# Sharing one sum of products between neighbouring pixels, in one batch of four, in a stack of location-dependent convolutions

## The chip, the cores and the metric

The kernel runs on one core of one Trainium2 chip. The metric is the time of one execution on the device in microseconds (us). A comparison counts from about 0.2% upwards.

## What is computed

Four layers work on an input of 4 batches, 32 x 32 pixels and 16 channels. Each layer normalises its input (a group norm over pairs of channels) and adds its result to it. The first three layers have this form, and nearly all of the work is in their `second` term: for each of the 1024 output pixels (i, j) there is a 3 x 3 convolution of its own, `K`, which runs over the whole image of every batch.

```
first = jnp.einsum('ijpq,bpqc->bijc', M2, inputs)
K = jnp.transpose(G, (2, 3, 4, 0, 1, 5)).reshape(kh, kw, c, h * w * f)
shifted = lax.conv_general_dilated(inputs, K, window_strides=(1, 1), padding='SAME', ...)
shifted = shifted.reshape(b, h, w, h, w, f)
diff = jax.nn.relu(inputs[:, :, :, None, None, :] - shifted)
second = jnp.einsum('ijpq,bpqijc->bijc', W2, diff)
return first - L * second
```

The fourth layer is a long filter that the kernel applies as products with a Toeplitz matrix.

## The kernel before, in words

A **block** is 8 output pixels with 16 channels each, so 128 columns of weights. A layer has 128 blocks. A **pass** is one block with one batch, and its result is a PSUM tile `pt` of 128 x 1024 values, two banks of 512. There are 3 x 128 x 4 = 1536 passes. Since relu(x - s) is -min(s - x, 0), the identity is taken off the middle tap of the weights (L495, on GpSimd), and one VectorE instruction per pass (L591, `scalar_tensor_tensor`) takes the minimum with 0, multiplies by `Wp` and adds up along the row into `acc`.

TensorE makes a pass out of six matmuls (L583). The upper and lower 64 rows of the array each work on one half of the 1024 positions, beside each other. Each half has 64 rows of input: four taps of 16 channels (weights `ga`), four more taps (`gb`), both in plain fp32 over 512 columns, and the ninth tap (`gn`) in fp32r over 480 columns. In the ninth, weights and image are each split into a high and a low piece, and the four products of pieces fill the 64 rows. In the records, one fp32 matmul shows as two weight loads and two matmuls, one fp32r matmul as one of each; so a pass has 10 records of each kind (`ga` 4, `gb` 4, `gn` 2).

PSUM is a ring of four such `pt` tiles[...]. The blocks of a layer are taken in groups of 8 (`GC`), in this order: the first 8 blocks for batches 0 and 1, the same for batches 2 and 3, then the blocks between, each for all four batches, and the last 8 again by pairs of batches. So the image of one pair of batches can be made while the other pair is worked on.

Beside that, short pieces of other work are written as generators, and `step()` advances each of them by one piece after each pass: the norm and the image of the next layer (`make_image`, `store_image`, `load_image`), which write the normalised image to DRAM and read it back shifted by the taps, on the queues of SP, ACT and POOL in turn (32 transfers for a pair of batches); the `first` term (L437); the filter of layer 4. The weights are fetched per 8 blocks by three transfers on SP's queue (L480), the middle tap is changed by GpSimd (L495), and the ninth tap is split by ScalarE (L499) and VectorE (L503). `Wp` comes by SP's queue (L522), 1 MB for two blocks, into a ring of six tiles.

Layer 0 starts from an array `raw` that the host has laid out by taps, so that its images are only loaded and normalised in place (`load_first`, `first_images`). Layer 4's Toeplitz tiles are loaded during layer 3 into `TB` = 5 tiles and some more, all but one of them.

Of the kernel before, what the change touches and what calls it, by code (L numbers as in the profile page):

```python
# [7 lines left out]
F32 = mybir.dt.float32  # L30
# [7 lines left out]
P = 128  # L38
B, C, S = 4, 16, 32
NBLK = 128  # L40
TAPS = [0, 1, 3, 4, 8, 5, 6, 7, 2], [0, 1, 3, 4, 2, 5, 6, 7, 8]
ROW = 2 * 4 * 34
RUN = ROW - 2
NINE = 2 * 4 * 32
GC = 8
# [7 lines left out]
TB = 5  # L53
# [3 lines left out]
def conv_stack_kernel(ctx, tc, x, raw, M, W, first_w, G, h0, coef, cst, dft, idp, idq, out):  # L57
# [8 lines left out]
    gp = ctx.enter_context(tc.tile_pool(name="gp", bufs=2))  # L66
    gs = ctx.enter_context(tc.tile_pool(name="gs", bufs=2))
# [12 lines left out]
    cs = const.tile([P, P + C + 2], F32, name="cs")  # L80
    nc.sync.dma_start(out=cs, in_=cst)
    nc.scalar.dma_start(out=xs, in_=x)
    avg, mid = cs[:, :P], cs[:, P : P + C]
    avg_r = const.tile([P, P], F32R, name="avg_r")
    is_lo, sign = cs[:, P + C : P + C + 1], cs[:, P + C + 1 :]

    ys, ye, img = [], [], []  # L90
    for a in range(2):
        ys.append(const.tile([P, ROW + 2 * NINE], F32, name=f"y{a}"))
        ye.append(const.tile([P, ROW + 2 * NINE], F32, name=f"e{a}"))
        img.append(dram.tile([10, C, ROW + 2 * NINE], F32, name=f"img{a}"))
# [6 lines left out]
    half_blks = NBLK // 2  # L101

# [73 lines left out]
    def image_tiles(a):  # L176


        ims[a] = [
            imp.tile([P, *shape], d, tag=f"im{a}{k}", name=f"im{a}{k}")  # L180
            for k, (d, shape) in enumerate(
                ((F32, (4, 2, 4, 34)), (F32, (4, 2, 4, 34)), (F32R, (2, 4, 4, S)))
            )
        ]

    def load_first(a, which, b=slice(0, 2)):

        if a not in ims:
            image_tiles(a)
            nine[a] = st.tile([P, 2, 4, 4, S], F32, name=f"nine{a}")  # L190
        src = raw[:, a, 4 * ROW * which :][:, : 4 * (NINE if which == 2 else ROW)]
        if which == 2:
            nc.sync.dma_start(
                out=nine[a][:, b].rearrange("p b l cc x -> p (b l cc x)"),
                in_=src[:, b.start * 2 * NINE : b.stop * 2 * NINE],
            )
            return
        to = ims[a][which]
        nc.sync.dma_start(
            out=to[:, :, b].rearrange("p l b cc x -> p l (b cc x)"),  # L200
            in_=src.rearrange("p (l b n) -> p l b n", l=4, b=2)[:, :, b].rearrange(
                "p l b n -> p l (b n)"
            ),
        )

    def first_images():


        of = lambda t, b: t[:, :, b % 2].rearrange("p l cc x -> p l (cc x)")
        rlo = st.tile([P, B], F32, name="rlo")  # L210

        def center(b):
            v = of(ims[b // 2][1], b)
            nc.scalar.activation(v, v, AF.Identity, bias=neg[:, b : b + 1])

        def scale(b):
            v = of(ims[b // 2][1], b)
            nc.scalar.activation(v, v, AF.Copy, scale=rstd[:, b : b + 1])

        def clear(which, a, b=slice(0, 2)):  # L220

            top, bottom = (0, 0, slice(0, S)), (3, 3, slice(0, S))
            t = ims[a][which].bitcast(F32)
            if which == 2:
                t = t.rearrange("p b l cc x -> p l b cc x")
            left, right = ((slice(0, 4), slice(0, 4), slice(x, x + 1)) for x in (0, S - 1))
            parts = {
                0: [(g, g + 16, left) for g in range(0, P, 32)] + [(0, 32, top)],
                1: [(g, g + 32, right) for g in (0, 64)]
                + [(g + 32, g + 48, left) for g in (0, 64)]  # L230
                + [(96, P, bottom)],
                2: [(0, P, right)],
            }[which]
            for lo, hi, (l, cc, x) in parts:
                nc.gpsimd.memset(t[lo:hi, l, b, cc, x], 0.0)  # L235

        def first_tap(b, which=0):
            v = of(ims[b // 2][which], b)
            nc.vector.tensor_scalar(v, v, neg[:, b : b + 1], rstd[:, b : b + 1], ALU.add, ALU.mult)  # L239

        def last_tap(b):

            v, v8 = (
                t[:, b % 2].rearrange("p l cc x -> p (l cc x)") for t in (nine[b // 2], ims[b // 2][2])
            )
            m = neg[:, b : b + 1]
            nc.vector.tensor_scalar(v8, v, m, rstd[:, b : b + 1], ALU.add, ALU.mult)
            yield
            nc.vector.tensor_scalar(v, v, m, rlo[:, b : b + 1], ALU.add, ALU.mult)
            yield  # L250
            nc.vector.scalar_tensor_tensor(v8, v8.bitcast(F32), sign, v, ALU.mult, ALU.add)
            clear(2, b // 2, slice(b % 2, b % 2 + 1))
# [14 lines left out]
        first, second = prepare_g(0, 0, halves[0], nc.vector), prepare_g(0, 0, halves[1])  # L267
        tables = [coefs[:, at : at + 2 * P].rearrange("p (r n) -> p r n", r=2) for at in soon_at]
        def dft(ch, ri):
            coefficient_dft(dfts[ch], ab, tables[ch], ri)  # L270
# [4 lines left out]

# [3 lines left out]
        norm = group_norm(xs, as_it_is, group_sums)  # L279
        next(norm)  # L280
        next(first)
        next(first)
# [3 lines left out]
        next(first)  # L286
# [7 lines left out]
        at = [slice(b % 2, b % 2 + 1) for b in range(B)]  # L294
# [4 lines left out]
        center(0)  # L299
        scale(0)  # L300
        for ch in range(1, SOON):
            result(ch)
        first_tap(0)
        clear(0, 0, at[0])
        clear(1, 0, at[0])
        nc.vector.tensor_scalar(rlo, rstd, is_lo, None, ALU.mult)
        list(first)
        list(last_tap(0))
        for which in range(2):
            first_tap(1, which)  # L310
            clear(which, 0, at[1])
        list(last_tap(1))
        next(second)

        def rest():

            yield
            yield
            list(second)
            yield  # L320
            center(2)
            center(3)
            clear(1, 1)
            yield
            for _ in range(3):
                yield
            for b in (2, 3):
                scale(b)
                first_tap(b)
                clear(0, 1, at[b])  # L330
                yield
                yield from last_tap(b)
                yield
            for a in range(2):
                normalise(a, xs[:, 2 * a : 2 * a + 2], *(t[:, 2 * a : 2 * a + 2] for t in (neg, rstd)))
                yield

            nc.vector.tensor_copy(avg_r, avg)

        todo.append(rest())  # L340

    def normalise(a, xt, neg, rstd):
        yc[a] = work.tile([P, 2, NBLK], F32, tag=f"yc{a}", name=f"yc{a}")
        for b in range(2):
            at = slice(b, b + 1)
# [67 lines left out]
    def first_term(layer, xt):  # L413

        ft = work.tile([P, 2, 8, S], F32, tag="ft", name="ft")
        with tc.tile_pool(name="mp", bufs=4) as mp:
# [15 lines left out]
            for _ in range(GC - 4):  # L432
                yield
# [699 lines left out]
```

## Time and profile before

| | us |
|---|---|
| median of 3 runs (3060.91 to 3060.95) | 3060.93 |
| the profiled execution, its own time | 3061.04 |
| its span, first to last instruction | 3059.2 |
| TensorE busy by the records | 3049.9 |
| VectorE busy | 2066.2 |
| GpSimd busy | 245.9 |
| ScalarE busy | 74.8 |

The page gives the busy time of each engine, the span in 40 slices, the DMA queues, the chain of work that ended last, the costliest groups (line, engine, operation, tiles, shapes, count, busy time, mean of one in ns, idle time before it and its releaser), and the DMA issues. The ends of matmuls are modelled, so their start times are to be trusted and their durations are not. A timeline merges neighbouring records of one kind into a row: start, time from the start of the first to the end of the last, and how many.

### The profile page before, as it was taken

How to read it: one execution, taken by the hardware profiler on the slowest of the kernel's cores; microseconds unless marked ns; L12 is line 12 of the kernel's file. 1: busy time of each engine (PE TensorE's matmuls, PEld its weight loads, DVE VectorE, ACT ScalarE, POOL GpSimd, SP SyncE). 2: the span in 40 equal slices, each digit the busy share in tenths (PEclk: the TensorE clock that was granted, in tenths of full speed). 3: DMA queues.
4: the chain of work that ended last, by engine and by line, in shares of the span. 5: the costliest groups of instructions: out<-in, count | busy, mean ns of one | idle time of the engine just before them, and what ended most of it. 6: DMA issues, size and time to landing. Idle time of an engine off the chain costs nothing.

```text
span 3059.2 us, 39208 instructions
## 1 busy us (share of the span) xinstructions
PE 3049.9 (100%) x16268; PEld 2080.0 (68%) x16268; DVE 2066.2 (68%) x3358; ACT 74.8 (2%) x97; POOL 245.9 (8%) x288
## 2 busy tenths in 40 slices
PE   9999999999999999999999999999999999999999
PEld 5656556788766885678876555588567887655554
DVE  7667766666667776666666666777666766666664
ACT  1000000000000000000000000000000000000000
POOL 1022320000000201000000000020100000000000
PEclk9999999999999999999999999999999999999999
DMA  7353443333432745333433343274544444445422
GB/s 236 101 148 90 111 116 94 90 90 97 104 90 62 159 131 131 90 90 97 103 90 90 97 104 90 62 156 131 143 101 99 102 115 107 97 96 119 99 41 43
DMA packets 72218, 322.20 MB, mean 105 GB/s; under 512 B 10920, under 2 KB 21160, under 8 KB 46696
## 3 DMA queue, kind: packets, MB, share of 16 engines
q1 hardware_dynamic: 60464, 302.09, 39.5%
q10 hardware_dynamic: 7112, 9.93, 1.8%
q0 software_dynamic: 4464, 7.68, 1.2%
q8 instruction: 127, 2.08, 0.3%
q14 instruction: 51, 0.42, 0.1%
HBM read 313.46 MB, written 6.20 MB: 104 GB/s over the span
## 4 chain that ended last, share of the span: by engine, by line
PE 99%; DVE 0%; DMA 0%; issue 0%; ACT 0%; POOL 0%; ACTq 0%; DVEq 0%
PE pt L583 97%; PE pt L863 1%; PE pt L437 1%; DMA g<-in_G_dram 0%; DVE junk L591 0%; PE pt L690 0%; PE pt L731 0%; PE pt L617 0%; POOL im L235 0%; DVE im L239 0%; DVE gn L503 0%; ACT gn L499 0%; DVE st L142 0%; ACT L781 0%; DVE x L606 0%
## 5 line engine op out<-in xcount | busy, mean ns | idle before, releaser
L591 DVE SCALAR_TENSOR_TENSOR junk<-pt,w 128x1024 f32<-128x1024 f32 x1536 | 1880.9, 1225 | 945.6 <-PE pt L583 923.8
L583 PE MATMUL pt<-im,ga 64*128 64x512 f32 x6144 | 1941.8, 588 | 0.1
L583 PE MATMUL pt<-im,gb 64*128 64x512 f32 x6144 | 1940.7, 588 | 0.0
L583 PE MATMUL pt<-im,gn 64*128 64x480 f32 x3072 | 1574.2, 778 | 0.0
L583 PEld LDWEIGHTS pt<-im,gb 64*128 64x128 f32 x6144 | 916.6, 186 | 418.0 <-issue 294.3
L583 PEld LDWEIGHTS pt<-im,ga 64*128 64x128 f32 x6144 | 919.6, 185 | 174.4 <-issue 68.8
L583 PEld LDWEIGHTS pt<-im,gn 64*128 64x128 f32 x3072 | 509.2, 186 | 334.9 <-issue 270.0
L495 POOL TENSOR_TENSOR ga<-ga,cs 128x1024 f32<-128x1024 f32 (+1 forms) x48 | 112.6, 2346 | 1990.3 <-DMA ga<-in_G_dram 1990.1
L591 DVE DVE_READ_ACCUMULATOR junk<-pt,w 128x1 f32 x1536 | 127.3, 83 | 0.0
L503 DVE TENSOR_TENSOR gn<-g,gn 32x1024 fp32r<-32x1024 f32 (+2 forms) x98 | 117.7, 1201 | 2.8 <-ACT gn L499 0.6
L499 ACT CAST gn<-g 128x1024 fp32r<-128x1024 f32 (+2 forms) x49 | 50.4, 1028 | 2225.5 <-PE pt L583 2120.0
L452 POOL DMA_DIRECT2D fd<-ft x48 | 25.3, 534 | 314.8 <-ACT ft L444 302.4
L863 PE MATMUL pt<-t,y 128*32 128x512 f32 (+3 forms) x352 | 23.9, 432 | 0.0
L405 POOL DMA_DIRECT2D im<-img x44 | 22.3, 513 | 17.2 <-DMA img<-y 9.8
L746 POOL COPY hs<-v 32x512 f32<-32x512 f32 x16 | 17.1, 1071 | 46.4 <-ACT v L740 45.8
L863 PEld LDWEIGHTS pt<-t,y 128*32 128x32 f32 x352 | 10.9, 110 | 12.8 <-issue 10.9
L987 DVE TENSOR_TENSOR xo<-xo,both 128x512 f32<-128x512 f32 x2 | 1.4, 692 | 23.7 <-DMA both<-sd 23.7
L661 POOL TENSOR_TENSOR H<-H,d 128x256 f32<-128x256 f32 x8 | 6.8, 849 | 91.1 <-DVE d L666 90.8
L863 PE MATMUL pt<-t,yp 128*32 128x512 f32 (+3 forms) x192 | 13.6, 434 | 0.0
L378 POOL COPY e<-y 32x204 f32<-32x204 f32 (+1 forms) x8 | 3.6, 481 | 117.4 <-ACT y L375 117.4
L863 PEld LDWEIGHTS pt<-t,yp 128*32 128x32 f32 x192 | 6.1, 110 | 7.4 <-issue 6.2
L437 PE MATMUL pt<-mt,yt 128*64 128x512 f32 x48 | 11.0, 598 | 0.0
(107 smaller groups left out, 197.9 us busy)
## 6 DMA issues: line engine op xcount, KB each, us to landing
w<-in_W_dram SPq DMA_DIRECT2D x188, 1024.0 KB, 7.2
g<-in_G_dram SPq DMA_DIRECT2D x47, 512.0 KB, 7.8
ga<-in_G_dram SPq DMA_DIRECT2D x47, 512.0 KB, 3.6
gb<-in_G_dram SPq DMA_DIRECT2D x47, 512.0 KB, 6.4
mt<-in_M_dram SPq DMA_DIRECT2D x12, 512.0 KB, 8.3
w<-in_M_dram SPq DMA_DIRECT2D x12, 512.0 KB, 3.7
t<-hd ACTq DMA_DIRECT2D x28, 160.0 KB, 7.0
t<-hd SPq DMA_DIRECT2D x28, 160.0 KB, 8.1
```

Source lines behind the costliest of these rows:

```text
L378: nc.gpsimd.tensor_copy(e[96:, :, 1:, :], v[96:, :, :3, :])
L405: (nc.sync, nc.scalar, nc.gpsimd)[n % 3].dma_start(out=out, in_=src.rearrange("l c x -> c l x"))
L437: nc.tensor.matmul(pf[64 * h : 64 * h + 64], lhsT=yt[:, k].rearrange("k b c -> k (b c)"), rhs=mt[:, bass.ts(h, 512)], start=(k == 0), stop ...
L452: nc.gpsimd.dma_start(out=fv[h, cc, b], in_=ft[at : at + C, cc])
L495: engine.tensor_tensor(gv, gv, mid.unsqueeze(1).to_broadcast([P, gv.shape[1], C]), ALU.subtract)
L499: nc.scalar.copy(gn, g9)
L503: nc.vector.tensor_tensor(lo, g9[r : r + 32], lo.bitcast(F32), ALU.subtract)
L583: nc.tensor.matmul(pt[:, half, px], lhsT=w[rows, blk % GC, :], rhs=rhs, start=n == 0, stop=n == 2,)
L591: nc.vector.scalar_tensor_tensor(junk, pt.rearrange("p h m -> p (h m)"), 0.0, wt, ALU.min, ALU.mult, accum_out=acc[b // 2][:, b % 2, blk : ...
L661: mul = lambda o, u, w: nc.gpsimd.tensor_tensor(o, u, w, ALU.mult)
L746: nc.gpsimd.tensor_copy(hs[quarter[u], :, bass.ts(c, 8)], v[quarter[c], bass.ts(u, 8)].rearrange("q p m -> q m p"),)
L863: nc.tensor.matmul(rows.rearrange("n (j r) -> n j r", j=C)[:, :, 8 * cc :], lhsT=y(cc).rearrange("p q b -> p (q b)"), rhs=ts[k][q][:, :, : ...
```

## The change

Pixels are taken in pairs of neighbours along a row. Call the left one's inputs x0, x1, x2 and the right one's x1, x2, x3, and a row of taps g0, g1, g2. With S = g0 + g1 + g2, the left sum is S·x1 + g0·(x0 - x1) + g2·(x2 - x1), and the right sum, over x1, x2, x3, is S·x1 + g1·(x2 - x1) + g2·(x3 - x1). So one product S·x1 per row of taps serves both pixels, and each has two products of its own.

- Batches 0 to 2 keep six matmuls per pass (`direct`), with other taps in the fours and with even and odd pixels apart.
- Batch 3 uses `shared`: six fp32r matmuls of 256 columns for the three S·x1, into a PSUM tile `both`; ScalarE copies `both` to SBUF (`sb`); then for even and for odd pixels six matmuls of 256 columns each into `pt`: two of four taps in fp32, four of one tap in fp32r. VectorE adds `sb` to `pt` in place, and the instruction with the minimum follows as before. A shared pass takes two tiles of the PSUM ring.
- The weights come per 4 blocks (`GC` = 4) in `prepare_g`: GpSimd changes the middle tap and makes S, ScalarE and GpSimd split S and the third tap into pieces, GpSimd's queue writes the pieces to DRAM by eight transfers, and SP's queue reads them back into six tiles by nine; the six tiles are double buffered. A list of pairs of passes (`units`, `first_need`, `last_use`) says when each begins.
- `raw` is gone: layer 0 makes its images as the other layers do, through DRAM. An image of batches 0 and 1 takes 36 transfers, one of batches 2 and 3 takes 76. `make_image` is spread over more steps.
- `TB` is 3; three Toeplitz tiles are loaded inside the last stage.

The core of the diff:

```diff
-TAPS = [0, 1, 3, 4, 8, 5, 6, 7, 2], [0, 1, 3, 4, 2, 5, 6, 7, 8]
-ROW = 2 * 4 * 34
-RUN = ROW - 2
-NINE = 2 * 4 * 32
-GC = 8
+SHARED = (False, False, False, True)
+FOURS = [[0, 3, 6, 5], [1, 4, 7, 8]], [[0, 3, 6, 5], [1, 4, 7, 2]]
+PX = 4 * S
+JOB = 8
+GC = 4
...
+    gs = ctx.enter_context(tc.tile_pool(name="gs", bufs=3))
+    gn = ctx.enter_context(tc.tile_pool(name="gn", bufs=2))
+    ge = ctx.enter_context(tc.tile_pool(name="ge", bufs=1))
...
+    units = []
+    for layer in range(3):
+        ends = range(JOB), range(NBLK - JOB, NBLK)
+        units += [(layer, blk, a) for a in range(2) for blk in ends[0]]
+        units += [(layer, blk, a) for blk in range(JOB, NBLK - JOB) for a in range(2)]
+        units += [(layer, blk, a) for a in range(2) for blk in ends[1]]
+    last_use = {}
+    for n, (layer, blk, _) in enumerate(units):
+        last_use[(layer * NBLK + blk) // GC] = n
...
+    def image_tiles(layer, b):
+        tile = lambda name, d, *shape: imp.tile([P, *shape], d, tag=f"{name}{b}", name=f"{name}{b}")
+        if SHARED[b]:
+            ims[layer, b] = [
+                tile("f", F32, 4, 2, 64),
+                tile("n", F32R, 4, 2, 64),
+                *(tile(name, F32R, 4, 64) for name in ("m", "v", "s0", "s1", "s2")),
+            ]
+        else:
+            ims[layer, b] = [tile("f", F32, 4, 2, PX), tile("n", F32R, 4, PX)]
...
+                v = yp[a][:, b].rearrange("p cc (m k) -> p cc m k", k=2)
+                here, after, m = v[:, :, :16, 1], v[:, :, 1:, 1], v[:, :, :, 0]
+                row = ys[:, b, : 9 * 64].rearrange("p (k cc m) -> p k cc m", k=9, m=16)
+                nc.gpsimd.tensor_tensor(row[:, 1], m[:, :, 1:], here, ALU.subtract)
+                nc.gpsimd.tensor_tensor(row[:, 2], after, here, ALU.subtract)
+                nc.gpsimd.tensor_tensor(row[:, 0], m[:, :, :16], here, ALU.subtract)
+                whole = ys[:, b, 64:192]
+                hi, lo = ys[:, b, 192:384], ys[:, b, 384:576]
+                yield
+                nc.scalar.copy(hi[:, 128:].rearrange("p (cc m) -> p cc m", m=16).bitcast(F32R), here)
+                yield
+                nc.scalar.copy(hi[:, :128].bitcast(F32R), whole)
+                nc.gpsimd.tensor_tensor(
+                    row[:, 8], here, hi[:, 128:].rearrange("p (cc m) -> p cc m", m=16), ALU.subtract
+                )
+                yield
+                nc.gpsimd.tensor_tensor(lo[:, :128], whole, hi[:, :128], ALU.subtract)
+                edges.append((b, row))
...
+    def prepare_g(q, wait=3):
+        layer, ch = divmod(q, NBLK // GC)
+        raw = ge.tile([96, 3, 2 * P], F32, tag="raw", name="raw")
+        nc.sync.dma_start(out=raw.rearrange("r k n -> r (k n)"), in_=E[layer][ch])
+        f = gs.tile([P, 2, GC * P], F32, tag="f", name="f")
+        nc.sync.dma_start(out=f.rearrange("r k n -> r (k n)"), in_=F[layer][ch])
+        yield
+        for _ in range(wait):
+            yield
+        fv = f[:, 1].rearrange("r (n f) -> r n f", f=C)
+        rv = raw[:, 1].rearrange("r (n f) -> r n f", f=C)
+        for v, m in ((rv, mid_e), (fv, mid)):
+            nc.gpsimd.tensor_tensor(
+                v, v, m.unsqueeze(1).to_broadcast([v.shape[0], v.shape[1], C]), ALU.subtract
+            )
+        for k in (1, 2):
+            nc.gpsimd.tensor_tensor(raw[:, 0], raw[:, 0], raw[:, k], ALU.add)
+        for _ in range(wait):
+            yield
+        both = raw[:, 0::2]
+        hi, lo = (ge.tile([96, 2, 2 * P], F32R, tag=tag, name=tag) for tag in ("hi", "lo"))
+        nc.scalar.copy(hi, both)
+        yield
+        nc.gpsimd.tensor_tensor(lo, both, hi.bitcast(F32), ALU.subtract)
+        to = gd[q % 3]
+        for k, t in enumerate((hi, lo)):
+            for u in range(2):
+                for slot in range(2):
+                    nc.gpsimd.dma_start(
+                        out=to[slot, :, k, :, bass.ts(u, 2 * P)],
+                        in_=t[48 * u : 48 * u + 48, slot].bitcast(F32),
+                    )
+        yield
+        while q > 1 and now["unit"] <= last_use[q - 2]:
+            yield
+        tiles = [gn.tile([P, GC * P], F32R, tag=f"g{n}", name=f"g{n}") for n in range(6)]
+        gt[q] = f, *tiles
+        for n, (slot, *dys) in enumerate(((1, 0, 2), (1, 2, 0), (1, 1), (0, 0), (0, 1), (0, 2))):
+            for half, dy in enumerate(dys):
+                rows = slice(64 * half, 64 * half + 64) if len(dys) > 1 else slice(0, P)
+                src = to[slot, dy].rearrange("k c n -> (k c) n")
+                nc.sync.dma_start(
+                    out=tiles[n][rows].bitcast(F32),
+                    in_=src.unsqueeze(0).to_broadcast([4 // len(dys), 32, GC * P]),
+                )
...
+    def shared(layer, blk, b):
+        f, n, m, v, *ws = gt[(layer * NBLK + blk) // GC]
+        at = bass.ts(blk % GC, P)
+        fi, ni, mi, vi, *sums = ims[layer, b]
+        both = pair_psum()[:, :, :256]
+        for dy, (w, t) in enumerate(zip(ws, sums)):
+            for half in range(2):
+                rows = slice(64 * half, 64 * half + 64)
+                nc.tensor.matmul(
+                    both[:, half],
+                    lhsT=w[rows, at],
+                    rhs=t[rows].rearrange("p l m -> p (l m)"),
+                    start=dy == 0,
+                    stop=dy == 2,
+                )
+        sb = small.tile([P, 2, 256], F32, tag="both_sb", name="both_sb")
+        nc.scalar.copy(sb, both)
+        pt = pair_psum()
+        taps = ((f[:, 0], fi[:, :, 0]), (n, ni[:, :, 0]), (m, mi)), ((f[:, 1], fi[:, :, 1]), (n, ni[:, :, 1]), (v, vi))
+        for k in range(2):
+            for j, (w, t) in enumerate(taps[k]):
+                for half in range(2):
+                    rows = slice(64 * half, 64 * half + 64)
+                    nc.tensor.matmul(
+                        pt[:, half].rearrange("p (r k m) -> p k r m", k=2, m=16)[:, k],
+                        lhsT=w[rows, at],
+                        rhs=t[rows],
+                        start=k == j == 0,
+                        stop=k == 1 and j == 2,
+                    )
+        v = pt.rearrange("p h (r k m) -> p (h r) k m", k=2, m=16)
+        nc.vector.tensor_tensor(
+            v,
+            v,
+            sb.rearrange("p h (r m) -> p (h r) m", m=16).unsqueeze(2).to_broadcast([P, 32, 2, 16]),
+            ALU.add,
+        )
+        return pt
+    def run_unit(n, acc):
+        layer, blk, a = units[n]
+        now["unit"] = n
+        for b in (2 * a, 2 * a + 1):
+            pt = (shared if SHARED[b] else direct)(layer, blk, b)
+            junk = junkp.tile([P, S * S], F32, tag="junk", name="junk")
+            nc.vector.scalar_tensor_tensor(
+                junk,
+                pt.rearrange("p h m -> p (h m)"),
+                0.0,
+                wts[64 * layer + blk // 2][:, blk % 2, :],
+                ALU.min,
+                ALU.mult,
+                accum_out=acc[a][:, b % 2, blk : blk + 1],
+            )
+            step()
...
+    first_need = {}
+    for q in range(2, 3 * NBLK // GC):
+        first_need.setdefault(last_use[q - 3] + 1 if q > 2 else 0, []).append(q)
...
-        w = np.asarray(inputs[f"L{i}_conv_Wp"]).reshape(4, 8, S, 4, 8, S)
-        w = w.transpose(0, 2, 1, 4, 3, 5).reshape(64, 2, 8, S * S).transpose(0, 2, 1, 3)
+        w = np.asarray(inputs[f"L{i}_conv_Wp"]).reshape(4, 8, S, 4, 8, S // 2, 2)
+        w = w.transpose(0, 2, 1, 4, 3, 6, 5).reshape(64, 2, 8, S * S).transpose(0, 2, 1, 3)
...
+        g = g.transpose(0, 2, 3, 4, 1, 5).reshape(NBLK // GC, GC, 9, C, P)
+        fours = [[g[:, :, taps].transpose(0, 2, 3, 1, 4) for taps in half] for half in FOURS]
+        fours = np.stack([np.stack(half, 3) for half in fours], 1)
+        arrays[f"F{i}"] = fours.reshape(NBLK // GC, P, 2 * GC * P)
+        e = g.reshape(NBLK // GC, 2, GC // 2, 3, 3, C, P).transpose(0, 1, 3, 5, 4, 2, 6)
+        arrays[f"E{i}"] = e.reshape(NBLK // GC, 96, 3 * GC // 2 * P)
...
-    held, last = (1, 0, 7, 6, 5, 4, 3), 2
-    after = (3, 7, 6, 5, 4)
+    held, last = (1, 7, 6, 0, 5), 2
+    after = (7, 6, 5, 4, 3)
...
-        if n == 2:
-            list(load_toeplitz(last, toeplitz_tile(last, tp)))
+        if n in (2, 4, 5):
+            k = {2: 4, 4: 3, 5: last}[n]
+            list(load_toeplitz(k, toeplitz_tile(k, tp)))
```

## Prediction

> **What bounds the kernel now.** I read the page's busy times first, then the chain of work that ended last, then the groups.
>
> ```profile
> PE 3049.9 (100%) x16268; PEld 2080.0 (68%) x16268; DVE 2066.2 (68%) x3358; ACT 74.8 (2%) x97; POOL 245.9 (8%) x288
> ...
> PE 99%; DVE 0%; DMA 0%; issue 0%; ACT 0%; POOL 0%; ACTq 0%; DVEq 0%
> ...
> L591 DVE SCALAR_TENSOR_TENSOR junk<-pt,w 128x1024 f32<-128x1024 f32 x1536 | 1880.9, 1225 | 945.6 <-PE pt L583 923.8
> L583 PE MATMUL pt<-im,ga 64*128 64x512 f32 x6144 | 1941.8, 588 | 0.1
> L583 PE MATMUL pt<-im,gn 64*128 64x480 f32 x3072 | 1574.2, 778 | 0.0
> L583 PEld LDWEIGHTS pt<-im,gn 64*128 64x128 f32 x3072 | 509.2, 186 | 334.9 <-issue 270.0
> L503 DVE TENSOR_TENSOR gn<-g,gn 32x1024 fp32r<-32x1024 f32 (+2 forms) x98 | 117.7, 1201 | 2.8 <-ACT gn L499 0.6
> L495 POOL TENSOR_TENSOR ga<-ga,cs 128x1024 f32<-128x1024 f32 (+1 forms) x48 | 112.6, 2346 | 1990.3 <-DMA ga<-in_G_dram 1990.1
> ```
>
> The chain is TensorE from end to end, and the conv matmuls never wait (idle 0.1 us over 6144). VectorE waits 924 us for them. So TensorE's time per pass decides. Matmul ends are modelled, so I take starts. In the timeline of TensorE and of its weight loads, a usual pass:
>
> ```profile
> 15.26 1.02 PE L583 MATMUL pt<-im,ga 64*128 64x512 f32 x4
> 16.12 1.02 PE L583 MATMUL pt<-im,gb 64*128 64x512 f32 x4
> 16.58 0.78 PE L583 MATMUL pt<-im,gn 64*128 64x480 f32 x2
> 17.20 0.59 PE L583 MATMUL pt<-im,ga 64*128 64x512 f32 x2
> ```
> ```profile
> 16.55 0.19 PEld L583 LDWEIGHTS pt<-im,gn 64*128 64x128 f32 x2 [0.24 <-issue]
> 16.98 0.41 PEld L583 LDWEIGHTS pt<-im,ga 64*128 64x128 f32 x4 [0.24 <-issue]
> ```
>
> A pass takes 17.20 - 15.26 = 1.94 us (1536 of them: 2980 us, the chain's 97%). `ga` to `gb` is 0.86: two records per half, 0.43 each, both halves beside each other. `gb` to the next `ga` is 1.08, so the ninth tap has 1.08 - 0.86 = 0.22. An fp32 record sends its 512 columns twice (0.43 / 1024 = 0.42 ns a column); at that rate 480 columns are 0.20. The slot is longer than its columns. The next weights' load starts with the ninth's matmul (16.12 + 0.86 = 16.98), and their matmul comes 0.22 later. Now two other places: fp32 matmuls of 256 columns (their loads), and a tiny fp32r matmul (8 columns) with `ga` behind it.
>
> ```profile
> 320.14 0.94 PEld L617 LDWEIGHTS pt<-coefs,table 64*128 64x128 f32 x8
> ```
> ```profile
> 1021.67 0.16 PE L122 MATMUL pt<-pieces,avg_r 64*128 64x8 f32 x1
> 1021.70 0.67 PE L583 MATMUL pt<-im,ga 64*128 64x512 f32 x1
> ```
> ```profile
> 1021.68 0.51 PEld L583 LDWEIGHTS pt<-im,ga 64*128 64x128 f32 x4
> ```
>
> L617's eight loads are (0.94 - 0.19) / 7 = 0.107 apart, the halves in turn: 0.215 per half, as long as 2 x 256 columns. After L122, `ga` really begins at 1021.70 + 0.67 - 0.59 = 1021.78, only 0.10 after its load. So a load costs 0.10 when its half of the array stands empty, and nothing I find is shorter than 0.215 when a matmul is running in it.
>
> **What the Trainium skill says.** "TensorE: Matmul & The Clock Gate", section "LDWEIGHTS (loading the stationary operand)", prices a load by its columns at 1.2 GHz: 107 ns for 128. The 0.10 above agrees. Its section "Back-to-back issue gap" says that load and matmul together set the spacing, and gives some 81 ns for 128 columns where the matmul alone would be 56; the trace has no such stream, but the 0.22 for 480 columns points the same way. "TensorEngine Tiling (Array Packing)", "Key Properties": tiles load and multiply in parallel. The trace agrees: the halves' loads show as one row of 0.19 for two.
>
> **The change, part by part** (against the profiled 3061.04 us, of which 3059.2 span; the median, 3060.93, is the same).
>
> *Passes of batches 0 to 2* keep two fp32 matmuls and one fp32r of 480 columns per half: 1.94, no change.
>
> *Passes of batch 3*, 384 of them. Per half: three fp32r matmuls of 256 columns, then twice one fp32 matmul (two records) and two fp32r. That is 4 fp32 records at L617's 0.215 = 0.86, and 7 fp32r slots. No row shows an fp32r matmul of 256 columns in a stream. From below it is its columns, 256 x 0.42 = 0.107; from above the load's 0.216 (the ninth tap's slot, which is longer than its columns). I take 0.216: in the ninth tap the load, not the columns, seems to end the slot, and here every load begins under a matmul. 7 x 0.216 + 0.86 = 2.37, so 2.37 - 1.94 = +0.43 x 384 = **+167 us**. At 0.107 it would be 1.61: -0.33 x 384 = -127. In columns alone the change saves a sixth of a pass; it has 22 loads per pass where there were 10.
>
> *VectorE*: +384 additions of 128 x 1024 out of PSUM, nearest row L591, 1.23 each: +472; L503's 118 go to GpSimd. 2066 + 472 - 118 = 2420 us. Per block 4 x 1.33 + 1.23 = 6.6 beside TensorE's 3 x 1.94 + 2.37 = 8.2: hidden. Where only batches 2 and 3 run (16 blocks a layer), 3.9 beside 4.3: hidden still. With a short shared pass (1.61) TensorE needs 3.55 there: 48 blocks x 0.35 = 17 us lost.
>
> *ScalarE*: +384 copies of 128 x 512, some 0.58 by the row of L632: hidden by the second part of the pass (1.7). *PSUM*: a shared pass takes two of four tiles; the copy frees the first, and the next use of it is two direct passes later.
>
> *Weights*, per 4 blocks (33 us): GpSimd 3 additions of 256 and two of 512 per row, by L495's 2.3 ns an element 4 us, and eight DMA issues at 0.53 (as L452), 4 us: 8 of 33. SP gets 11 issues of some 0.35. Bytes per block grow from 0.72 to about 1.2 MB, in packets of 1 to 4 KB; the DMA share goes from some 0.4 to 0.6. `Wp` is asked for 8 blocks ahead. ScalarE's split waits for GpSimd, which waits for the fours, which wait for TensorE's end with the tile three groups back; behind it on ScalarE stand the copies for VectorE. It comes 8 passes (16 us) after the issue, against 8 for landing (`g` 7.8) and 4 for GpSimd: covered by 4 us. Uncovered, it would cost what it is late, once per 4 blocks. Cost taken: nothing.
>
> *Start*. Conv matmuls begin at 10.66 now. Then: norm ready at 9.2, image to its store 3.7 (between the same steps at 992.7 and 996.35 now), store 2.6, 18 transfers for the first batch on three queues 3.2, landing 4.8: 23.5, and GpSimd's eight weight writes ahead of its copies, 4: 27.5. **+17** (13 to 25).
>
> *Layer ends*. The image loads are now issued at
>
> ```profile
> 998.98 2.64 SPq L405 DMA_DIRECT2D im<-img  x5
> 999.00 3.04 ACTq L405 DMA_DIRECT2D im<-img  x5
> 999.47 4.54 POOL L405 DMA_DIRECT2D im<-img  x9 [2.52 <-DMA img<-y]
> ```
>
> 0.5 each. For batches 2 and 3 there are 76, 25 a queue: 13 us. The last piece of VectorE's image comes some 12 passes into the 16 (31 us) of batches 0 and 1: 23 + 3 for the store + 13 + 5 = 44, where batch 3 is due at 33. About 9 us lost in each of three layers. The image of batches 0 and 1 is just about ready (twice 2 to 4 us; its ScalarE issues also hold back copies). With 3 us for the late Toeplitz tiles: **+35** (5 to 60).
>
> Sum: 3061 + 167 + 17 + 35 = **3280 us**.
>
> **Rivals.** *A, the above*: 0.216 per fp32r slot. Range 3240 to 3325. Chance 0.50.
>
> *B, faster*: the load hides even under 256 columns, and the 0.02 in the ninth's slot is some fixed extra. Slots of 0.107 to 0.127: -127 to -73, with +52 and VectorE's +17: 2990 to 3050, say 3010. For it: fp32 records follow each other without a gap although each has a load; against: all those are 0.215 or longer. It wins below (1.94 - 52 / 384 - 0.86) / 7 = 0.135 per slot. Chance 0.28.
>
> *C, between*: a load runs at half speed under a matmul and at full speed after it: 0.107 + 0.05 = 0.16; 7 x 0.16 + 0.86 = 1.98, +15, +52: 3130. Chance 0.16.
>
> *D, the copies are late*: DMA is busier, the fours land in 15 instead of 8 us, ScalarE's split holds the copies, VectorE and then PSUM stop TensorE for 3 us in each of 96 groups: +290 on A: 3570. For it: one queue carries all of this; against: 4 us of cover and a DMA share of 0.6. Chance 0.06.
>
> **How the numbers follow.** Faster by more than 0.2% (what a measurement can tell here) is B, less its upper edge: 0.27. Within 0.2%: 0.03, where B and C meet. Slower: 0.70. The range 3005 to 3325 leaves out D and the better half of B, under 0.2; A's own range stands above.
>
> **What would show it.** In the profile after, the shared fp32r matmuls' loads of one half 0.21 to 0.22 apart (A), 0.11 to 0.13 (B), 0.16 (C); a block every 8.2 us in mid-layer; the chain still TensorE; the first conv matmul near 27 us; gaps at the three layer starts before batch 3. Wrong: TensorE idle in mid-layer for ScalarE, or shared passes under 1.8 us.

## The result, and the profile after

| | before | after |
|---|---|---|
| median of 4 runs, us | 3060.94 (3060.91 to 3061.59) | 4643.2 (4638.6 to 4650.02) |
| span of the profiled execution, us | 3059.2 | 4648.2 |
| TensorE busy, us | 3049.9 | 3228.6 |
| VectorE busy, us | 2066.2 | 2411.6 |
| first conv matmul, us | 10.66 | 55.31 |

The kernel became slower by half: the ratio is 1.517 (95% interval 1.5144 to 1.5197). The forecast was 3280 with a range of 3005 to 3325.

The lines of the page of the kernel after that answer to those shown of before: the busy times, the granted clock in 40 slices, the chain of work that ended last by engine and by line, and three groups.

```profile
PE 3228.6 (69%) x20876; PEld 1927.1 (41%) x20876; DVE 2411.6 (52%) x3644; ACT 301.9 (6%) x543; POOL 1065.0 (23%) x1545
...
PEclk7878888888888877888888888887788888888889
...
DMA 22%; PE 17%; SPq 13%; POOL 4%; issue 2%; DVE 1%; ACT 1%; ACTq 0%; POOLq 0%; DVEq 0%
DMA f<-in_F_dram 20%; PE pt L498 14%; SPq L450 9%; SPq L412 3%; PE pt L528 2%; POOL raw L425 2%; POOL f L421 1%; DMA t<-hd 1%; ACT both_sb L521 1%; DVE junk L550 1%; PE pt L513 0%; PE pt L845 0%; DMA g<-gd 0%; DMA img<-ye 0%; DVE pt L536 0%
...
L498 PE MATMUL pt<-f,f 64*128 64x512 f32 x9216 | 2396.3, 637 | 1297.2 <-ACT both_sb L521 1089.6
...
L536 DVE TENSOR_TENSOR pt<-pt,both_sb 128x1024 f32<-128x1024 f32 x384 | 473.1, 1232 | 1583.6 <-ACT both_sb L521 1379.2
...
L430 ACT CAST hi<-raw 96x512 fp32r<-96x512 f32 x96 | 59.3, 617 | 2079.9 <-POOL raw L425 2079.9
```

The chain was TensorE for 99%; now no engine has half of it. Its largest piece is one load, the fours `f` from DRAM, 20%, and SP's queue has 13% more. TensorE stands idle 1090 us ahead of L498 for ScalarE's copy (L521), and VectorE waits for the same copy. ScalarE itself is busy 6% only. It waits 2080 us, ahead of the split of L430, for GpSimd. So the page names ScalarE, and the chain names a DMA; one group of four blocks shows how they hang together. (`F` is the array of the taps in fours, `E` holds the nine taps row by row, from which S is made; SP loads a piece of each once per group, into `f` and `raw`.) The timelines of the kernel after, here of SP's queue, of GpSimd, of ScalarE and of TensorE:

```profile
2435.09 0.54 SPq L414 DMA_DIRECT2D f<-in_F_dram  x1
2435.73 2.25 SPq L471 DMA_DIRECT2D w<-in_W_dram  x2
2463.89 12.70 SPq L450 DMA_DIRECT2D g<-gd  x8
2476.69 2.42 SPq L412 DMA_DIRECT2D raw<-in_E_dram  x1
2479.16 0.54 SPq L414 DMA_DIRECT2D f<-in_F_dram  x1
...
2451.89 1.26 POOL L421 TENSOR_TENSOR f<-f,cs 128x512 f32<-128x512 f32 x1 [0.61 <-DMA f<-in_F_dram]
...
2458.93 2.36 POOL L437 DMA_DIRECT2D gd<-lo  x4
...
2454.65 0.62 ACT L430 CAST hi<-raw 96x512 fp32r<-96x512 f32 x1 [20.57 <-POOL raw L425]
2455.18 0.57 ACT L521 COPY both_sb<-pt 128x512 f32<-128x512 f32 x1
...
2443.41 0.80 PE L498 MATMUL pt<-n,g 64*128 64x480 f32 x2
2455.81 3.79 PE L498 MATMUL pt<-f,f 64*128 64x512 f32 x8 [11.59 <-ACT both_sb L521]
2500.40 3.79 PE L498 MATMUL pt<-f,f 64*128 64x512 f32 x8 [12.01 <-ACT both_sb L521]
```

Read in order of time: SP issues `f` at 2435.1. It lands nearly 17 us later, GpSimd begins with it at 2451.9, the split runs on ScalarE at 2454.65, and only behind it the copy that TensorE has been waiting for since 2444.2: it frees a PSUM tile for the second pass of the next block. Then the pieces go to DRAM, SP reads them back (eight transfers, 12.7 us of issuing), and behind these stands the next `f`, at 2479.16. (The read-backs of a group are these eight; the count of nine, in the description of the change, in the prediction's 11 issues and in one expectation below, is one too many.) From one `f` to the next are 44.1 us. TensorE's own work for four blocks is 30. A loop of waits that runs round once per group sets the time.

### The profile page after: what moved, and what is told of

Same layout as the page of the kernel before. It is cut to its first block, busy times and chain, and to the rows that moved or that the text cites. A ratio compares the mean times of both kernels' runs of the same rounds, so it can differ in the third digit from the quotient of the medians.

```text
span 4648.2 us, 53283 instructions
## 1 busy us (share of the span) xinstructions
PE 3228.6 (69%) x20876; PEld 1927.1 (41%) x20876; DVE 2411.6 (52%) x3644; ACT 301.9 (6%) x543; POOL 1065.0 (23%) x1545
## 4 chain that ended last, share of the span: by engine, by line
DMA 22%; PE 17%; SPq 13%; POOL 4%; issue 2%; DVE 1%; ACT 1%; ACTq 0%; POOLq 0%; DVEq 0%
DMA f<-in_F_dram 20%; PE pt L498 14%; SPq L450 9%; SPq L412 3%; PE pt L528 2%; POOL raw L425 2%; POOL f L421 1%; DMA t<-hd 1%; ACT both_sb L521 1%; DVE junk L550 1%; PE pt L513 0%; PE pt L845 0%; DMA g<-gd 0%; DMA img<-ye 0%; DVE pt L536 0%
## 5 line engine op out<-in xcount | busy, mean ns | idle before, releaser
L498 PE MATMUL pt<-f,f 64*128 64x512 f32 x9216 | 2396.3, 637 | 1297.2 <-ACT both_sb L521 1089.6
L498 PEld LDWEIGHTS pt<-f,f 64*128 64x128 f32 x9216 | 972.0, 203 | 2140.4 <-ACT both_sb L521 1140.4
L536 DVE TENSOR_TENSOR pt<-pt,both_sb 128x1024 f32<-128x1024 f32 x384 | 473.1, 1232 | 1583.6 <-ACT both_sb L521 1379.2
L498 PE MATMUL pt<-n,g 64*128 64x480 f32 x2304 | 985.7, 820 | 7.3 <-DMA g<-gd 7.3
L421 POOL TENSOR_TENSOR raw<-raw,cs 96x256 f32<-96x256 f32 x96 | 68.7, 715 | 3188.8 <-DMA raw<-in_E_dram 3188.8
L528 PE MATMUL pt<-f,f 64*128 64x256 f32 x3072 | 477.9, 383 | 5.8 <-DVE junk L550 3.6
L528 PE MATMUL pt<-n,g 64*128 64x256 f32 x1536 | 375.9, 471 | 0.0
L498 PEld LDWEIGHTS pt<-n,g 64*128 64x128 f32 x2304 | 251.7, 199 | 291.6 <-issue 280.9
L521 ACT COPY both_sb<-pt 128x512 f32<-128x512 f32 x384 | 224.0, 583 | 2089.6 <-PE pt L513 1936.6
L528 PEld LDWEIGHTS pt<-f,f 64*128 64x128 f32 x3072 | 252.3, 190 | 6.7 <-DVE junk L550 3.8
L437 POOL DMA_DIRECT2D gd<-hi x384 | 229.8, 604 | 4.9 <-issue 4.8
L437 POOL DMA_DIRECT2D gd<-lo x384 | 226.7, 597 | 1.8 <-issue 1.8
L430 ACT CAST hi<-raw 96x512 fp32r<-96x512 f32 x96 | 59.3, 617 | 2079.9 <-POOL raw L425 2079.9
L528 PEld LDWEIGHTS pt<-n,g 64*128 64x128 f32 x1536 | 160.2, 191 | 14.0
```

The lines of the kernel that those rows point to most:

```text
L421: nc.gpsimd.tensor_tensor(v, v, m.unsqueeze(1).to_broadcast([v.shape[0], v.shape[1], C]), ALU.subtract)
L437: nc.gpsimd.dma_start(out=to[slot, :, k, :, bass.ts(u, 2 * P)], in_=t[48 * u : 48 * u + 48, slot].bitcast(F32),)
L498: nc.tensor.matmul(pt[:, half, px], lhsT=w[rows, at], rhs=rhs, start=k == 0, stop=k == 2)
L521: nc.scalar.copy(sb, both)
L528: nc.tensor.matmul(pt[:, half].rearrange("p (r k m) -> p k r m", k=2, m=16)[:, k], lhsT=w[rows, at], rhs=t[rows], start=k == j == 0, stop= ...
L536: nc.vector.tensor_tensor(v, v, sb.rearrange("p h (r m) -> p (h r) m", m=16).unsqueeze(2).to_broadcast([P, 32, 2, 16]), ALU.add,)
```

## The experiments

Two theories at the start. **L**: the preparation of the weights is one serial loop through SP's queue (read-backs, `E` and `F` behind them, GpSimd, split, pieces, read-backs), and the read-backs themselves make it long, since each of them is spread over few DMA engines. **H**: ScalarE is the fault; the split, which waits for GpSimd, stands in front of the copies. Each kernel has its own line numbers; ScalarE's copy, L521 in the kernel after, is L519 or L516 in some of them.

**1. The split on GpSimd** (`e_cast_pool`).

```diff
-        nc.scalar.copy(hi, both)
+        nc.gpsimd.tensor_copy(hi, both)
```

> The cast that splits the weights moves from ScalarE to GpSimd, so nothing stands before ScalarE's copies any more. Theory L (a serial loop of the weights' preparation through SP's queue, 44.5 us per 4 blocks, sets the time): the loop is as long as before, 4550 to 4750 us. Rival H (ScalarE, held by that cast, sets the time): 3000 to 3400 us.

Measured: 4551.85 us (one run). The waits of TensorE in this kernel (total, times, longest):

```profile
PE pt L513 <- DMA g<-gd: 748.9, 195, 7.5
...
PE pt L498 <- ACT both_sb L521: 172.1, 16, 26.9
```

The wait for the copies fell from 1090 to 172 us, and most of it came back as a wait of 749 us for the tiles `g`; the kernel gained 2%. H falls: the name beside TensorE's wait was the last link, and not what makes the loop long.

**2. All batches direct** (`e_direct`).

```diff
-SHARED = (False, False, False, True)
+SHARED = (False, False, False, False)
```

> Batch 3 is computed like the others (no shared pass, no copy, no addition), while all weights are still prepared, split, written and read back. Theory L: 4400 to 4700 us, since the loop is untouched. Rival H: no copies to hold, so 3100 to 3200 us.

Measured: 4471.22 us (one run). There is no shared pass, no copy and no addition left, and the time is within 4% of the kernel after; TensorE waits 754 us for `g`. The preparation of the weights is enough to make the kernel this long.

**3. The read-backs in pieces of 32 rows** (`e_spread`): 24 transfers from 32 rows to 32 rows, where there were eight from 32 rows repeated 4 or 2 times.

```diff
-                nc.sync.dma_start(
-                    out=tiles[n][rows].bitcast(F32),
-                    in_=src.unsqueeze(0).to_broadcast([4 // len(dys), 32, GC * P]),
-                )
+                for r in range(rows.start, rows.stop, 32):
+                    nc.sync.dma_start(out=tiles[n][r : r + 32].bitcast(F32), in_=src)
```

> The read-back of the split weights is issued as 24 transfers of 32 rows in place of 8 whose slowest dimension is a repeat of 4 or 2; the bytes are the same. Theory L with few DMA engines as its cause: each transfer can use all engines, the backlog goes, the fours land in some 8 us, the loop falls to about 30 us per 4 blocks: 3000 to 3250 us. If the loop is long for the bytes or for SP's issuing alone: 4300 to 4900 us.

Measured: 3330.11 us (3328.95 to 3334.89), ratio 1.0877 (1.0859 to 1.0896). Nearly all of the loss is gone, with the same bytes and more transfers. L expected 3000 to 3250, so it was too hopeful by 80 us.

**4. The same with all batches direct** (`e_spread_direct`).

> As e_spread, with batch 3 computed like the others. Beside e_spread it prices the shared pass. If shared passes take 1.69 us as the trace of after shows and TensorE sets the time: 384 x 0.25 = 96 us more than e_spread. If they took the 2.37 that was predicted: 167 us less than e_spread.

Measured: 3227.41 us (3222.36 to 3231.77), ratio 1.0543 (1.0527 to 1.0558). A miss: I expected it to be 96 us slower than `e_spread`, and it is 103 faster. The next run shows why. SP's queue in `e_spread`:

```profile
1699.83 11.65 SPq L451 DMA_DIRECT2D g<-gd  x23
1711.58 0.36 SPq L412 DMA_DIRECT2D raw<-in_E_dram  x1
1711.99 0.43 SPq L414 DMA_DIRECT2D f<-in_F_dram  x1
```

`E` and `F` are still issued behind all read-backs of the group before. The loop is now about as long as TensorE's 30 us, so that a disturbance reaches TensorE: it still waits 127 us for copies.

**5 and 6. `E` and `F` ahead of the read-backs** (`e_order`), **and that with all batches direct** (`e_order_direct`). `e_order` is `e_spread` with

```diff
-                    todo.extend(prepare_g(q) for q in first_need.get(n, ()))
+                    todo[:0] = [prepare_g(q) for q in first_need.get(n, ())]
```

> The kernel of e_spread with one more change: the preparation of a new group goes to the head of the list of side work, so that SP issues its loads of E and F ahead of the 24 read-backs of the group before, and not behind them. L, made exact by the two runs before (what holds TensorE is one serial loop per group, read-backs issued on SP for 12 us, then F landing, then ScalarE's split in front of the copies): F's issue no longer waits for the read-backs, the split is there long before ScalarE needs it, and the waits of TensorE for the copies in mid-layer go to nothing. Groups of 4 blocks then take 4 x 7.49 = 30.0 us; 96 x 30.0 = 2876, with some 77 for the other conv-free stretches and the last layer, 35 to 45 at the start and 30 to 50 at each of three layer ends: 3050 to 3200. If what is left in e_spread was not the loop but the mass of transfers itself (F landing late because the DMA engines are busy) it stays at 3300 to 3360.

> The kernel of e_order with all four batches direct (SHARED all False): the preparation of weights stays, nothing uses its six tiles but the ninth tap's, ScalarE has no copies and VectorE no additions. It prices the shared pass by itself, now without the loop: if TensorE sets the time in both, a shared pass of 1.69 us against 1.94 gives 384 x 0.25 = 96 us, so this one is 70 to 120 us slower than e_order (3130 to 3300). If batch 3's passes take what the prediction said (2.37), it is 165 faster than e_order. If the loop still holds e_order, it is faster than e_order by 30 or more, as it was between e_spread_direct and e_spread.

Measured: `e_order` 3176.63 us (3176.0 to 3178.58), ratio 1.0377 (1.0359 to 1.0394); `e_order_direct` 3182.04 (3180.07 to 3183.3), ratio 1.0394 (1.0379 to 1.041). SP's queue and ScalarE in `e_order`:

```profile
1726.77 0.36 SPq L414 DMA_DIRECT2D f<-in_F_dram  x1
1727.36 11.32 SPq L451 DMA_DIRECT2D g<-gd  x24
...
1710.68 0.59 ACT L519 COPY both_sb<-pt 128x512 f32<-128x512 f32 x1 [6.88 <-PE pt L511]
1711.16 0.62 ACT L430 CAST hi<-raw 96x512 fp32r<-96x512 f32 x1
1718.17 0.59 ACT L519 COPY both_sb<-pt 128x512 f32<-128x512 f32 x1 [6.39 <-PE pt L511]
```

`F` goes first, the split no longer waits for anything, and each copy waits for TensorE alone. TensorE's wait for copies is down to 34 us, and in the last two thirds of a layer the blocks follow each other every 7.49 us. L holds within its range. But the second half missed: the shared passes save 96 us over four direct ones (7.49 for 7.74 in 384 blocks), and the two kernels differ by 5. The gaps of TensorE, from the starts and ends in the records, say where it went: between the start and the last stage `e_order` has 107 us in gaps of 0.8 us or more, `e_order_direct` 54. And TensorE's busy time is 3010.3 against 3073.8, which is 64 apart and not 96, so some 32 us are passes that ran longer in `e_order`. The gaps lie at the layer ends and in the first third of each layer, where the images come late and the split still holds copies.

**7. The number of DMA engines by itself** (`e_flat`). This is the kernel after, with its eight read-backs, its order and its bytes; only the rows that are read are others. The ninth taps and the sums of batch 3 are then made with other weights, so that nothing but its time is of use.

```diff
-                src = to[slot, dy].rearrange("k c n -> (k c) n")
+                src = to.rearrange("s d k c n -> (s d k c) n")
-                nc.sync.dma_start(
-                    out=tiles[n][rows].bitcast(F32),
-                    in_=src.unsqueeze(0).to_broadcast([4 // len(dys), 32, GC * P]),
-                )
+                nc.sync.dma_start(out=tiles[n][rows].bitcast(F32), in_=src[rows])
```

> The changed kernel, with nothing but the source of the nine read-backs altered: each reads as many consecutive rows of the pieces in DRAM (128 or 64 rows of 2 KB) as it fills, and not 32 rows repeated four times or twice. Same number of transfers, same bytes, same packets of 2 KB, same waits; the values in the six tiles are other ones, so the ninth taps and the sums of batch 3 are computed from wrong weights. L with few engines as its root (a source whose slowest dimension is a repeat of 4 or 2 is spread over few DMA engines): the issues fall from 2.45 us to 0.3 to 0.6, F lands in 5 to 9 us, the loop is shorter than TensorE's 30 us per group, and the time falls to 3120 to 3300. If the cause is the mass of packets, or reading back what was just written, nothing changes: 4500 to 4700.

Measured: 3190.83 us (3184.67 to 3196.72), ratio 1.0424 (1.0408 to 1.0439). This change of the source is worth 1452 us. SP's queue in `e_flat`, and then the stretch in which one set of read-backs is issued: its length, the busy us of PE, PEld, DVE, ACT and POOL, each with its instructions, the granted clock, the DMA share and GB/s. First in `e_flat`:

```profile
1701.60 4.47 SPq L450 DMA_DIRECT2D g<-gd  x8
1706.17 0.36 SPq L412 DMA_DIRECT2D raw<-in_E_dram  x1
1706.58 0.43 SPq L414 DMA_DIRECT2D f<-in_F_dram  x1
```
```profile
1701.60:1706.10 4.50, 4.50 (x25) 3.37 (x23) 4.08 (x6) 0.00 (x0) 0.00 (x0) 1.00 0.52 151
```

and in the kernel after:

```profile
2464.00:2476.60 12.60, 12.60 (x82) 7.10 (x79) 10.94 (x15) 0.59 (x1) 0.00 (x0) 1.00 0.19 67
```

While the reads of the repeated source are issued, the DMA share is 0.19, three of 16 engines, at 67 GB/s; with rows in sequence it is 0.52 and 151. Eight issues take 4.5 us instead of 12.7, and `f` lands in 8.0 us (the median of `e_flat`'s DMA issues) instead of the 17 seen above. The Trainium skill has this rule: "DMA: Bandwidth & Descriptors", section "🎯 Rules for kernel authors", says that the size of the outermost dimension limits how many engines a transfer gets, "e.g. a leading zero-stride broadcast of c copies — confines the whole DMA to at most c engines". Here c is 4 for the full tiles and 2 for the halves; the three engines' worth of share agrees.

The trace's records of single packets show the rest. In the kernel after, the 768 read-back packets of 2 KB of the set above run from 2465.2 to 2493.6, 28.4 us of a loop of 44, with 2.9 in flight on the mean. In `e_flat` a set runs from 1702.9 to 1710.7, with 10 in flight. One packet takes 0.11 us in both, so the packets are not slower; fewer run beside each other. They are also what holds up `f`. Of the 128 packets of the `f` issued at 2435.09, 112 start between 2436.6 and 2440.4, and the last 16 only between 2449.2 and 2451.1, when the last read-back packet of the group before has ended (2448.9). The records don't number the engines.

**8 and 9. What is left: SP's queue at the start and the layer ends** (`e_yield`), **and then the split on GpSimd** (`e_yield_pool`). `e_yield` is `e_order` with a `yield` after the read-backs of each tile, so that one tile goes out per step, and with the image loads of the first two batches moved in front of all tiles but the first:

```diff
-        list(first)
+        next(first)
         load_image(0, 0)
+        list(first)
```

> The kernel of e_order with the 24 read-backs of a group issued tile by tile, one tile per step, and not in one piece; at the start the image loads of batches 0 and 1 go in front of all tiles but the first. In e_order the store of the next image stood 6 us behind 24 read-backs on SP's queue (1058.9 to 1064.9), and the first image loads 19 us. If that queue is what the layer ends and the start are late by: first conv at 34 to 38 for 44.3, each layer end 5 to 10 us shorter, total 3176.6 less 8 less 15 to 30: 3120 to 3160. If the 36 and 76 image transfers themselves set the gaps: 3165 to 3180.

> The kernel of e_yield with the split of L430 on GpSimd, so that ScalarE has nothing of the weights in front of its copies. In e_order TensorE stood for the copies behind the split 8 times in the early part of the layers, 34 us in all (3.0, 6.9 and 2.9 in layer 1). If these are left in e_yield, they go here: 10 to 35 us less than e_yield, 3090 to 3140. If GpSimd's extra 1.3 us per group or a wait of its queue matters, no gain or a few us more.

Measured: `e_yield` 3177.3 us (3176.87 to 3177.36), ratio 1.0379 (1.0362 to 1.0397): no gain over `e_order`. The first conv matmul did come at 35.75 instead of 44.70, but group 1's tile and the image of batches 2 and 3 were then late by as much. `e_yield_pool`: 3161.27 (3156.26 to 3164.39), ratio 1.0326 (1.031 to 1.0341): 16 us less than `e_yield`, which lies in the 10 to 35 expected of the split. The time itself was expected at 3090 to 3140, on top of a gain of `e_yield` that did not come.

**10 and 11. The image made at once** (`e_image`), **and that with all batches direct** (`e_image_direct`). In `store_image` five lines `yield` are taken out; at the start, group 1's `E` and `F` go first and group 0's later tiles are issued beside the passes.

> The kernel of e_yield_pool with the making of the image no longer spread: the five stops inside store_image are gone, so its operations follow each other in one step; and at the start E and F of group 1 are issued ahead of the tiles of group 0, of which only the first goes ahead of the image loads, the others one by one beside the passes. In e_yield_pool each layer began with a gap of TensorE of 14.8 us, and 4.7 more at batches 2 and 3; four stops of 1.94 us are 7.8 us. If the spread of the image is what the layer ends are late by: about 8 us less of the one and all of the other, 25 us for two layers, some 6 more since TensorE's clock is at half after such a gap, and 15 to 20 at the start: 3100 to 3135. If the transfers set the gaps whatever the image does (36 for batches 0 and 1, 76 for 2 and 3), only the start gains: 3140 to 3160. In neither case is it under 3061.

> The kernel of e_image with all four batches direct: the shared pass priced again, where little else stands in its way. Blocks of 7.49 us against 4 x 1.935 = 7.74 give 96 us over 384 blocks; the waits of batch 3 for its many image transfers (6 us in each layer) and the time in which VectorE is the slower one take 20 to 50 of them. So 45 to 80 us slower than e_image. If the shared passes gained nothing it would be within 10 us, as e_order_direct was of e_order.

Measured: `e_image` 3145.64 us (3144.86 to 3147.56), ratio 1.0277 (1.0259 to 1.0296); `e_image_direct` 3174.66 (3172.86 to 3177.21), ratio 1.0369 (1.0351 to 1.0388). `e_image` gained 16 us and fell in its second case, the transfers: the gaps of TensorE at a layer end add up to 25 or 26 us in `e_yield_pool` and in `e_image` alike, and most of the gain lies in the opening of layer 0, whose gaps shrank from 35 to 23 us. The shared pass is worth 29 us and not the 45 to 80 expected. The layer end in `e_image`, ScalarE and VectorE:

```profile
1050.83 5.26 ACTq L345 DMA_DIRECT2D f<-img  x2
...
1062.09 1.07 ACT L516 COPY both_sb<-pt 128x512 f32<-128x512 f32 x2 [18.54 <-DMA g<-gd]
...
1062.71 1.23 DVE L531 TENSOR_TENSOR pt<-pt,both_sb 128x1024 f32<-128x1024 f32 x1 [13.17 <-ACT both_sb L516]
```

The image is ready earlier, so its loads are issued earlier, on ScalarE too. They take up to 5 us for two, and the copies of the shared pass stand behind them: TensorE stood still for 11.8 us there.

**12. No image loads on ScalarE at the layer ends** (`e_two_queues`).

```diff
-            (nc.sync, nc.scalar, nc.gpsimd)[n % 3].dma_start(out=to, in_=src)
+            queues = (nc.gpsimd, nc.sync) if a == 0 and layer else (nc.sync, nc.scalar, nc.gpsimd)
+            queues[n % len(queues)].dma_start(out=to, in_=src)
```

> The kernel of e_image, but at the end of a layer the 36 image loads of batches 0 and 1 are issued by GpSimd and SP only, 18 each, and none by ScalarE. In e_image TensorE stood 11.8 us at the end of each of two layers for a copy of the shared pass, which stood on ScalarE behind 12 image loads: two of them took 5.26 us to issue, and the copies waited 18.5 us. If those issues are what TensorE waits for: this gap goes, the last passes of batches 2 and 3 run through, and in its place TensorE waits for the image itself, 18 issues of 0.5 to 0.6 us on GpSimd and landing, some 3 to 8 us: 3145.6 less 2 x (4 to 9) less 2 x 3 for the clock: 3120 to 3138. If the image's arrival sets the layer end anyway and the copy only hides it: 3140 to 3155.

Measured: 3146.12 us (3142.66 to 3149.29), ratio 1.0277 (1.026 to 1.0295): no gain, the second case. TensorE and SP's queue at the layer end:

```profile
1066.18 3.75 PE L494 MATMUL pt<-f,f 64*128 64x512 f32 x6 [7.46 <-DMA f<-img]
...
1047.44 11.75 SPq L448 DMA_DIRECT2D g<-gd  x8
1059.88 1.13 SPq L346 DMA_DIRECT2D n<-img  x2
```

The wait for the copy is gone, a wait of 7.5 us for the image is in its place, and the next gap, before batches 2 and 3, grew from 7.2 to 12.4. The last store of the image was issued by 1045.5; SP's half of the loads begins only at 1059.88, since eight of the read-backs stand in front of them and took 11.75 us to issue. In that time SP waits for the landing of `Wp`, `E` and `F` (3.5, 0.8 and 3.5 us). So the choice of queue moves the wait. That the crowd of transfers at that point sets the layer end is my reading; what it would be without the read-backs in front was not tried. No version here beats the kernel before.

## Why the prediction was wrong, step by step

- **The failed step** is "Weights, per 4 blocks", with its "Cost taken: nothing". It gave SP "11 issues of some 0.35" (they are ten), `f` "8 for landing", and a cover of 4 us. Measured: 12.7 us for eight of the issues, 17 us for landing. Its numbers were those of transfers that the kernel before had, and no transfer of the kernel before repeats its source along the outermost dimension; with rows in sequence (`e_flat`) the landing is 8.0, as the prediction took it. The step also missed that the loop closes: `E` and `F` of the next group stand behind the read-backs on the same queue, so being late is not paid once but carried round. The price: a disturbed group lasts 44.6 us (2500.40 - 2455.81) where four blocks of 7.49 last 30. Of the 1589 us between the two spans, TensorE's idle time has 1410 (4648.2 - 3228.6, less 3059.2 - 3049.9), most of it the 1090 us of waits for the copies.
- **Rival D** named the right sign, ScalarE's split in front of the copies, and even a landing of 15 us. Its reason was a busier DMA on one queue, not reads that use few engines. It had 3 us per group and 3570 in all, at a chance of 0.06, because it took the cover as given and saw no loop. And `e_cast_pool` shows that its mechanism, ScalarE, was only the last link.
- **"Passes of batch 3"**: 0.216 per fp32r slot was wrong, and rival B's 0.107 to 0.127 right. TensorE's timeline of the kernel after, one block with its shared pass:

```profile
2463.81 1.88 PE L498 MATMUL pt<-f,f 64*128 64x512 f32 x8
...
2469.61 0.52 PE L513 MATMUL pt<-s,g 64*128 64x256 f32 x6
2469.96 0.60 PE L528 MATMUL pt<-f,f 64*128 64x256 f32 x4
...
2471.30 1.03 PE L498 MATMUL pt<-f,f 64*128 64x512 f32 x4
```

Three slots take 2469.96 - 2469.61 = 0.35, so 0.117 each. The pass takes 1.69 (predicted 2.37), the block 2471.30 - 2463.81 = 7.49 (predicted 8.2). The term is not +167 but -96. The load of the next weights does hide under 256 columns. So the 0.02 in the ninth tap's slot was not what the prediction took it for, a load that ends it.
- **VectorE and ScalarE**: right. 473.1 us of additions at 1232 ns (predicted 472), 2411.6 in all (2420), the copy 583 ns (0.58); hidden in mid-layer, where `e_order`'s blocks keep 7.49. The prediction gave the copy two direct passes before its PSUM tile is used again; in the lines of the result TensorE stops after one.
- **Start**: +17 predicted, +45 measured. In the kernel after, the first eight read-backs stand in front of SP's image loads; in `e_order` it is still +34, in `e_yield` +25.
- **Layer ends**: +35 predicted (44 less 33 is 11 a layer, where it took 9). `e_order` shows it cleanest. From its first conv matmul to the last stage it takes 68.7 us more than before (3114.2 - 44.70 against 3011.48 - 10.66) although its passes save 96, so 165 go to the layers, 107 of them in gaps of TensorE. The rest of the 165 fits the next point: TensorE's busy time in `e_order` is 3010.3, where 3049.9 - 96 = 2954 was due, so 56 us are passes that ran longer. The last stage, costed 3 us, takes 14.8 more.
- **A term that was not there**: what a gap costs after it has ended. After a gap of some 12 us TensorE runs at half its clock. The stretches of the kernel after with busy times and granted clock (the last column but two), in such a gap, behind it and undisturbed:

```profile
2447.00:2455.80 8.80, 0.00 (x0) 0.00 (x0) 0.01 (x1) 1.10 (x2) 3.82 (x5) 0.50 0.27 81
2455.80:2460.60 4.80, 4.79 (x12) 2.20 (x14) 4.25 (x6) 0.00 (x0) 4.80 (x8) 0.50 0.21 47
...
2463.80:2471.30 7.50, 7.50 (x57) 4.54 (x55) 6.17 (x9) 0.59 (x1) 0.00 (x0) 1.00 0.13 42
```

The first eight matmul records take 3.79 us, later ones 1.88, and the eight between them 2.29. The Trainium skill, "TensorE: Matmul & The Clock Gate", section "What's actually happening", has it: half the clock after an idle window of about 3.4 us, and about 3.4 us of work to come back. The trace agrees on the half; the times are others in this gap: the clock falls 2.7 us after TensorE stops (at 2444.2) and is back 4.8 us after it starts again. At 2.3 us each (3.79 + 2.29 - 2 x 1.88), the 82 waits for the copies in the kernel after make 189 of the 275 us by which TensorE's busy time exceeds 2954.

With the loop shorter than TensorE's 30 us, the change is a loss of 3 to 4%: in `e_order` the shared passes save 96 us, and start, layer ends and last stage take about twice that. `e_flat`, `e_order` and the versions built on it, with the shared pass, lie between 3145 and 3191 us. How much of the layer ends could be had back with fewer, larger image transfers stays open.

## What to carry to other kernels

When a change adds transfers, look at the outermost dimension of its source before pricing it by a transfer that the profile has; a repeat in that place made the issue of eight reads take 12.7 us instead of 4.5 here. Trace new waits as a loop: if the next round's loads stand on the same queue behind this round's results, lateness is not covered but sets the period. And the engine that a wait names may be the last link: one run that moves its work elsewhere tells whether it is more.

## What the runs showed of the hardware that was not expected

- A read-back of 128 rows from 32 rows repeated four times held SP's queue 2.58 us in one issue, and the unrelated `E` behind it 2.42; from rows in sequence, `E` took 0.36. The last 16 packets of the 128 of `f` started 9 us after the others, behind the read-backs' packets.
- Per half of the array, fp32r matmuls of 256 columns, each with its own weights, follow each other every 0.117 us. Their columns alone take 0.107 at the 0.42 ns that the kernel before shows.
- A gap of TensorE costs its length and then about 2.3 us more, since some 4.8 us run at half the clock.
